# Moving a policy product, four groups of transposes and four stores in a two-layer adaLN/FFN kernel

## The chip, the cores and the metric

The kernel runs on one core of a Trainium2 chip. The metric is the device time of one execution in microseconds (us); less is better. The engines are TensorE (PE; its weight loads are shown as PEld), VectorE (DVE), ScalarE (ACT), GpSimd (POOL) and SyncE (SP). SP, ACT and POOL also issue DMAs from their own queues, each strictly in the order of its program.

## The reference

The input x is 32 sequences of 128 tokens of 512 numbers (4096 tokens), in fp32. Two layers follow each other, `x = x + ffn(cond(x))`, and the part that matters here is the first one and the start of the second:

```
# layer 0, cond: a shared FFN plus the two best of 8 small experts per token
shared = silu(x @ sw1.T) * (x @ sw3.T) @ sw2.T            # 512 -> 1024 -> 512
routed = g0 * expert_a(x) + g1 * expert_b(x)              # gates from a sigmoid router
hid    = (shared + routed) / 3
# layer 0, ffn: one of 8 big experts per sequence, chosen by the last token
logits = gelu(hid[:, -1] @ Wp1 + bp1) @ Wp2 + bp2         # "policy"
sel    = argmax(softmax(logits))
h      = gelu(hid @ W1[sel] + b1[sel]);  out = (h @ W2[sel] + b2[sel]) @ Wo + bo
x1     = x + hid + 0.3 * out
# layer 1, cond: token shift (xk, xr), 16 hashed experts, sigmoid(xr @ w_recept) gate
# layer 1, ffn: a gated recurrence over the 32 sequences' axis, solved step by step
```

## The kernel before

Every fp32 product is made of three products of a split operand: a high part (a cast on ACT) and a low part (a subtraction on DVE). `split` makes the two parts and `mm3` the three products per 128 rows of depth, so PE sees long runs of 12 or 48 products.

The program is traced once, straight on, and a scheduler turns the trace into one fixed order per engine. It takes instructions whose inputs it models as ready, older ones first, so an instruction can move against those that are traced around it. Two means set that order by hand: `tc.issue_after(ins)` puts what is traced within it behind `ins` on the same engine, and a manual dependency of class NoSync does the same for a single pair. Neither adds a wait on the chip.

The tokens come in 32 blocks of 128 (one sequence each), in 8 groups of 4. The stages around the change:

- **Shared FFN, second half** (`shared` over groups 4 to 7, up to 820 us in the trace). For each n = 8 g + c it runs `up(n)`: two runs of 12 products, `p0_n` and `p1_n`, with `mid(n, w)` (here `between`) called after each run; then `down(n - 1)`, then `hook2(g, c)`. `up` sends the sums through ACT and DVE (`sg`, then its split parts `as`), and `down` uses these. `between` and `hook2` place `combine(b)`, which adds a block's shared sum and its two gathered expert rows `o` on DVE (L831, L832), turns the result on PE (four transposes into `pth`), scales it on ACT (L837), stores it (`hid_d` from ACT's queue, `xh_d` from SP's) and keeps the last token's column in `hl`. `get_o` gathers the rows of a later block from POOL's queue, and loads shared sums and x from SP's.
- **Policy, early part.** In `hook2` of the last group's first step (n = 56) `policy(0, 24)` is traced for 24 sequences: product `pol`, Gelu on ACT, a multiplication on DVE (`pr`), a second product `pl` with a matrix of ones that adds over partitions, and then a chain of small DVE operations that sorts the sequences by expert and gives the row indices `idxw` by which POOL gathers the experts' weights (`rawB`). The PSUM pool for `pth`, `pol` and `pl` has one buffer here.
- **End of the shared FFN.** `keep` copies the last group's four sums on ACT (L1053). These four blocks are not combined yet; their sums are stored to `sh_d` (L1056) and read back later.
- **Sequence stage** (820 to 1400 us). Step b runs `up(b+1, "a")` (tiles `pu`), two products `pv` (`send_v`) at every second step, `turn_r(b-1)` (`pr`), `down(b, "a")` (`po`, against W2a), `bend(b+1, "a")` (transposes `pt`, Gelu, split), at the other steps `send_k` (`ptB`), then the same for half b, and every second step `close` (`pb`, the product with Wo, and DVE work). Weights of the next expert are split within a branch that is taken only when a sequence has another expert than the one before. `pt`, `pr`, `ptB`, `pth`, `pol` and `pl` share two PSUM buffers. Three steps apart, `get_o` and then `combine` treat the last four blocks (28 to 31), and three steps later `policy(24, 32)` follows:

```
            late, step = divmod(b - 3, 3)
            if 0 <= late < GB and step == 0:
                with tc.issue_after(last_hid[0]), tc.issue_after(last_w[0]):
                    get_o(NB - GB + late, cb, 1)
...
                with behind(last_split), tc.issue_after(last_turn[0]):
                    if 0 <= late < GB and step == 2:
                        combine(NB - GB + late, ps_t)
                    if late == GB and step == 0:
                        policy(PARTS[0], NB, cb, ps_t)
```

The buffers of `get_o` are single here, so the next block's gathers wait until `combine` has let go of them. `used()` moves the queue of weights on by one: it splits the weights three places ahead and gathers those six places ahead.

The functions that the change touches, with what calls them:

## Time and profile before

| | us |
|---|---|
| median of 3 runs (lowest to highest) | 2436.91 (2435.3 to 2438.0) |
| profiled execution | 2437.49 |
| its span, from the first to the last instruction | 2435.8 |
| busy in the span: PE / PEld / DVE / ACT / POOL | 2399.1 / 2031.1 / 1488.7 / 1079.3 / 413.6 |
| mean granted TensorE clock | 0.997 |
| PE waits in all for: the late `pth` / `pt_0a` / `pl` | 2.5 / 2.2 / 2.1 |

The trace gives, for each engine, the start and length of every instruction in us from the start of the span. In the rows of the timeline, equal neighbours are merged (x12); what stands in brackets is the idle time of that engine just before, and the instruction or DMA that ended it. ACTq and SPq are issues of DMAs from those queues. The granted clock is TensorE's, as a share of full speed.

### The profile page before, as it was taken

The page shows a single profiled execution, that of the slowest core. Times are in us where ns is not written, and L with a number is a line of the kernel's source. Part 1 is how long each engine was busy: PE and PEld are TensorE (multiplying, and loading weights), DVE is VectorE, ACT ScalarE, POOL GpSimd, SP SyncE. Part 2 cuts the span into 40 slices and gives each one's busy share as a digit, 9 for nine tenths or more (in the row PEclk, how much of TensorE's full clock was granted, in tenths as well). Part 3 has the DMA queues.
Part 4 walks back from the last instruction along what each step waited for, and adds up shares of the span by engine and source line. Part 5 has one row for each costly group of instructions (what it writes and reads, how often), then busy time and mean ns, then how long its engine had stood idle before and what let it go on. Part 6 is the DMA issues. An engine that isn't in the chain of part 4 may idle for free.

```text
span 2435.8 us, 36814 instructions
## 1 busy us (share of the span) xinstructions
PE 2399.1 (98%) x12792; PEld 2031.1 (83%) x12792; DVE 1488.7 (61%) x2548; ACT 1079.3 (44%) x1897; POOL 413.6 (17%) x461
## 2 busy tenths in 40 slices
PE   8999999999999999999999999999999999999999
PEld 6788888888888787888888889999988888888887
DVE  8797644456557445446355476767756666666664
ACT  5544633344223545455355466666643233223242
POOL 1000022222233233232222110000010000000012
PEclk9999999999999999999999999999999999999999
DMA  6445555457575234343243287776641111111175
GB/s 214 148 130 171 180 173 165 154 168 256 180 222 185 92 119 138 105 125 115 74 153 131 73 309 230 221 234 225 219 152 61 44 52 50 48 47 48 52 233 182
DMA packets 196382, 357.93 MB, mean 147 GB/s; under 512 B 37664, under 2 KB 70480, under 8 KB 193632
## 3 DMA queue, kind: packets, MB, share of 16 engines
q1 hardware_dynamic: 147648, 257.53, 32.4%
q0 software_dynamic: 36448, 75.95, 10.9%
q10 hardware_dynamic: 12096, 22.03, 2.5%
q8 instruction: 107, 1.75, 0.3%
q14 instruction: 83, 0.68, 0.1%
HBM read 377.08 MB, written 91.80 MB: 192 GB/s over the span
## 4 chain that ended last, share of the span: by engine, by line
PE 51%; DMA 2%; DVE 1%; ACT 1%; issue 0%; POOL 0%; DVEq 0%; ACTq 0%; POOLq 0%
PE phD L82 7%; PE poD L82 7%; PE ps_f L82 7%; PE po L82 4%; PE poF L82 3%; PE ps_c L82 3%; PE pS L82 3%; PE ps_i L82 3%; PE pA L82 2%; PE pb L82 2%; PE pv L82 2%; PE ptD L1431 1%; PE ptC L1599 1%; PE ptF L1574 1%; PE ptB L1256 0%; DMA rawB<-in_W2b_dram,idxw 0%
## 5 line engine op out<-in xcount | busy, mean ns | idle before, releaser
L65 DVE TENSOR_TENSOR wD<-rawD,wD 128x1024 fp32r<-128x1024 f32 x128 | 156.6, 1230 | 82.1 <-ACT wD L64 82.0
L82 PE MATMUL p<-xhl,swu 128*128 128x512 f32 x768 | 190.4, 399 | 5.8 <-ACT xhl L64 5.8
L82 PEld LDWEIGHTS phD<-xe,wD 128*128 128x128 f32 x1536 | 185.1, 189 | 2.2 <-ACT xe L64 1.1
L82 PE MATMUL phD<-xe,wD 128*128 128x256 f32 x1536 | 185.9, 281 | 0.7 <-ACT xe L64 0.7
L82 PE MATMUL p<-xhl,kept_u 128*128 128x512 f32 x768 | 184.3, 394 | 0.7 <-DVE kept_u L65 0.7
L82 PE MATMUL poD<-wD,hD 128*128 128x512 f32 x768 | 181.5, 392 | 0.0
L82 PEld LDWEIGHTS p<-xhl,swu 128*128 128x128 f32 x768 | 145.7, 192 | 36.6 <-ACT xhl L64 5.8
L82 PEld LDWEIGHTS p<-xhl,kept_u 128*128 128x128 f32 x768 | 141.9, 188 | 30.0 <-DVE kept_u L65 1.1
L82 PEld LDWEIGHTS poD<-wD,hD 128*128 128x128 f32 x768 | 141.9, 188 | 28.3
L64 ACT CAST wD<-rawD 128x1024 fp32r<-128x1024 f32 x128 | 133.3, 1046 | 56.4 <-PE poD L82 54.0
L290 POOL DMA_INDIRECT xg<-in_x_rows_dram,blk_t x71 | 67.8, 954 | 446.5 <-PE ptx L300 246.6
L1542 POOL DMA_INDIRECT y<-res_d,gat_i x32 | 35.2, 1100 | 473.4 <-DVE r L1566 389.5
L82 PE MATMUL pur<-r,xb 128*128 x792 | 110.3, 288 | 4.1 <-ACT hbr L64 1.5
L65 DVE TENSOR_TENSOR xb<-ptx,xb 128x512 fp32r<-128x512 f32 x68 | 47.0, 691 | 105.8 <-ACT xb L64 104.1
L82 PE MATMUL por<-r,hbr 128*128 x396 | 108.0, 407 | 1.1 <-ACT hbr L64 1.1
L82 PEld LDWEIGHTS pur<-r,xb 128*128 128x128 f32 x792 | 98.3, 188 | 6.5 <-issue 2.2
L82 PE MATMUL ps_c<-uc_hl,cT 128*128 128x512 f32 x384 | 96.6, 399 | 0.1
L82 PE MATMUL pb<-rT,Wo_hl 128*128 128x256 f32 x768 | 95.2, 281 | 0.3 <-DVE rT L65 0.2
L815 POOL DMA_INDIRECT o<-o_d,s_i x64 | 66.0, 1031 | 170.3 <-PE pth L835 81.2
L82 PE MATMUL acc<-swd,as 128*128 128x512 f32 x384 | 94.2, 391 | 0.2 <-DVE as L65 0.2
L82 PE MATMUL ps_f<-wf_hl,z 128*128 128x512 f32 x384 | 94.4, 394 | 0.0
L82 PE MATMUL pv<-w_recept_hl,xr 128*128 128x512 f32 x384 | 93.1, 391 | 0.0
(1048 smaller groups left out, 5135.3 us busy)
## 6 DMA issues: line engine op xcount, KB each, us to landing
rawD<-in_w_key_dram SPq DMA_DIRECT2D x64, 512.0 KB, 4.1
rawD<-in_w_value_dram SPq DMA_DIRECT2D x64, 512.0 KB, 3.9
swr<-in_sw_dram SPq DMA_DIRECT2D x120, 256.0 KB, 3.5
o_d<-obr SPq DMA_DIRECT2D x66, 256.0 KB, 2.5
rraw<-in_rw_dram SPq DMA_DIRECT2D x32, 256.0 KB, 3.2
xc<-in_x_dram SPq DMA_DIRECT2D x32, 256.0 KB, 3.5
hid_d<-o ACTq DMA_DIRECT2D x32, 256.0 KB, 2.6
xh_d<-xc SPq DMA_DIRECT2D x32, 256.0 KB, 3.1
```

The costliest lines, as they stand in the source:

```text
L64: first = nc.scalar.copy(hi, src).ins
L65: done = nc.vector.tensor_tensor(lo, src, hi.bitcast(F32), ALU.subtract).ins
L82: done = nc.tensor.matmul(ps, lhsT=left(hl, k), rhs=right(hr, k), start=start and k + n == 0, stop=stop and 3 * k + n == last,)
L290: nc.gpsimd.indirect_dma_start(out=xg[i], out_offset=None, in_=a["x_rows"], in_offset=bass.IndirectOffsetOnAxis(ap=blk_t[:, i : i + 1], ax ...
L815: nc.gpsimd.indirect_dma_start(out=o[n], out_offset=None, in_=o_d, in_offset=bass.IndirectOffsetOnAxis(ap=idx[:, b : b + 1], axis=0),)
L1431: nc.tensor.transpose(pt[:, k, :], xe[:, s, bass.ts(k, P)], ident)
L1542: got = nc.gpsimd.indirect_dma_start(out=y, out_offset=None, in_=res_d, in_offset=bass.IndirectOffsetOnAxis(ap=gat_i[:, b : b + 1], axis=0),)
L1574: nc.tensor.transpose(pt[:, k, :], r[:, bass.ts(k, P)], ident)
L1599: nc.tensor.transpose(pt[:, k, :], c[:, bass.ts(k, P)], ident)
```

## The change

Three things are done. The second product of both policies, `pl`, is collected in a list `later`. In the early policy, the list is queued behind the last product of `p1_57`, the second run of the step after policy is traced. In the sequence stage, `hold_back()` follows every `down(b, "a")`, so the late policy's `pl`, and the four transposes of each of the four late `combine` calls (`held=True`), stand on PE behind the product with W2a of the next step. No wait is added on the chip; only PE's order is bound. Third, the four stores of the last group's shared sums are issued from SP's queue instead of ACT's.

The dependency that was written out at the last loop (`last_ob`) becomes a call of the new helper and is the same as before.

```diff
-    last_split = []
+    last_split, last_product, later = [], [], []
+
+    def queue_behind(ins, other):
+
+        tc.add_manual_dep(
+            ins, other.name,
+            mybir.DependencyInfo(mybir.DependencyClass.NoSync, mybir.DependencyReason.DATA),
+            reason="issue_after",
+        )
+
+    def hold_back():
+
+        while later:
+            queue_behind(later.pop(), last_product[0])
...
                     start=start and k + n == 0, stop=stop and 3 * k + n == last,
                 )
+        last_product[:] = [done.ins]
         return done.ins
...
-        def combine(b, ps_t):
+        def combine(b, ps_t, held=False):
...
             for k in range(KD):
-                nc.tensor.transpose(pt[:, k, :], o0[:, bass.ts(k, P)], ident)
+                turned = nc.tensor.transpose(pt[:, k, :], o0[:, bass.ts(k, P)], ident)
+                if held:
+                    later.append(turned.ins)
...
-            mm(pl, ones, pr, True, True)
+            later.append(nc.tensor.matmul(pl, lhsT=ones, rhs=pr, start=True, stop=True).ins)
...
                 if w == 0:
                     sums(*divmod(n - 1, KF))
+                elif n == last * KF + 1:
+                    hold_back()
...
-                        nc.scalar.dma_start(out=sh_d[i * P : (i + 1) * P, :], in_=shs[b])
+                        nc.sync.dma_start(out=sh_d[i * P : (i + 1) * P, :], in_=shs[b])
...
                 down(b, "a")
+                hold_back()
                 used()
...
                     if 0 <= late < GB and step == 2:
-                        combine(NB - GB + late, ps_t)
+                        combine(NB - GB + late, ps_t, True)
```

More of the change, by code (lines that the diff above doesn't have):

```diff
@@ L1703, in tile_kernel @@
         for ob in last_ob:
-            tc.add_manual_dep(
-                ob, last_split[0].name,
-                mybir.DependencyInfo(mybir.DependencyClass.NoSync, mybir.DependencyReason.DATA),
-                reason="issue_after",
-            )
+            queue_behind(ob, last_split[0])
         i0, i1 = (raw_part("wi", h) for h in range(2))
```

## The prediction

> **What bounds the kernel now.** I read the page first, then the waits of PE, then the timeline around each wait that the diff touches, then the windows with the granted clock. The page's first part:

> ```profile
> PE 2399.1 (98%) x12792; PEld 2031.1 (83%) x12792; DVE 1488.7 (61%) x2548; ACT 1079.3 (44%) x1897; POOL 413.6 (17%) x461
> ```

> TensorE is busy for 2399.1 of 2435.8 us, so a change that leaves the products alone can win only idle PE time, 36.7 us in all, and time that PE spends at a lowered clock. The waits of PE (total, times, longest) hold three rows whose instructions the diff moves or relieves:

> ```profile
> PE pth L835 <- DVE o L832: 2.5, 2, 2.3
> PE pt_0a L1151 <- ACT ue_0a L1144: 2.2, 1, 2.2
> PE pl L56 <- DVE pr L865: 2.1, 2, 1.3
> ```

> That is 6.8 us of PE idling. A stop costs a little more than its idle figure, because the last product's tail, which otherwise overlaps the next one, is exposed. So I take each loss from start to start, at the steady price of twelve 512-column products, 2.77 us (0.23 each), and 0.118 for a 256-column one (48 in 5.66), as the chain of waits shows them.

> **The stores of the last shared sums.** The timeline of before, where the shared FFN ends and the sequence stage begins:

> ```profile
> 821.58 3.00 ACTq L1056 DMA_DIRECT2D sh_d<-shc  x2
> ...
> 822.97 1.29 PE L82 MATMUL pu_0b<-wB_W1b,hidhl 128*128 128x512 f32 x5
> ...
> 824.62 1.04 ACT L64 CAST wB_W2b<-rawB 128x1024 fp32r<-128x1024 f32 x1 [2.59 <-DMA hidB<-hid_d]
> ...
> 825.78 0.59 ACT L1144 COPY ue_0a<-pu_0a 128x512 f32<-128x512 f32 x1
> ...
> 826.42 0.66 PE L1151 MATMUL pt_0a<-ident,ue_0a 128*128 128x128 f32 x4 [2.16 <-ACT ue_0a L1144]
> 826.83 3.13 PE L82 MATMUL pu_0b<-wB_W1b,hidhl 128*128 128x512 f32 x7
> ```

> ACT copies the last sum at 822.03. Its fourth store is issued only at 824.26, behind a wait that the landing of a hidB load ends, and in the same queue stand the second half of W2b's cast, then ue_0a, then PE. With the stores on SP, ACT goes on at 822.03: cast to about 823.1, ue_0a to 823.8. PE's five products of pu_0b end at 824.26, so pt_0a finds its input there. PE loses from 822.97 + 5 x 0.23 = 824.12 to 826.42, 2.30 us, and all of it should go.

> A second loss follows it; the windows (PE busy, PEld, DVE, ACT, POOL, granted clock, DMA):

> ```profile
> 824.00:827.00 3.00, 0.84 (x7) 0.58 (x6) 1.23 (x1) 2.24 (x3) 0.00 (x0) 1.00 1.03 371
> 827.00:831.00 4.00, 4.00 (x12) 3.13 (x11) 0.00 (x0) 2.92 (x7) 2.64 (x3) 0.57 0.81 292
> 831.00:835.00 4.00, 4.00 (x21) 3.28 (x20) 1.53 (x3) 2.89 (x8) 1.36 (x2) 1.00 0.23 66
> ```

> The granted clock falls to 0.57 right behind the stop: 4.00 x 0.43 = 1.72 us, and from starts (7 products in 2.93 and 7 in 1.96 instead of 1.61 each) 1.67. I count 1.67 with the stop. Against it: the equal stop at 929 us is followed by a clock of 1.00, so one stop in two has this price, and the term lies between 0 and 1.67; I take the upper end since this execution paid it. [...]

> What SP takes over: four issues of some 0.33 us each, and the wait for a landing. Behind them in SP's queue stand hidB of the third and fourth sequence (issued at 820.43 and 822.11), xB and Wo. The third hidB is cast at 831.01 and used by pu_2a at 842.34; Wo is cast at 850.74. If SP holds until 824.3 instead of 822.1, with 4.5 us to landing, hidB is there at 829. Nothing is lost; if that cover went, each us beyond would cost one.

> **The late sums' transposes.** Four groups lie in the stream of PE, at 929.88, 985.20, 1041.56 and 1096.86. The worst:

> ```profile
> 926.11 1.52 PE L82 MATMUL pv<-w_recept_hl,xr 128*128 128x512 f32 x6
> ...
> 928.99 0.75 DVE L832 SCALAR_TENSOR_TENSOR o<-o,g,o 128x512 f32<-128x512 f32 x1 [0.21 <-DVEq L990]
> ...
> 929.88 0.63 PE L835 MATMUL pth<-ident,o 128*128 128x128 f32 x4 [2.25 <-DVE o L832]
> ...
> 932.10 3.02 PE L82 MATMUL po<-wB_W2a,hb_6a 128*128 128x512 f32 x12
> ```

> From starts: 926.11 + 6 x 0.23 = 927.49 against 929.88, 2.39 lost. At 1041.56 six pv from 1039.78, 0.40; at 985.20 and 1096.86, 36 pb from 980.64 and 1092.30 (4.25 us), 0.31 each. Sum 3.41. The change puts each group behind the next po (W2a): after 935, 993, 1047 and 1105 in the old clock of the trace, where o has been ready for 5 us or more. What comes late with it: ACT's copy, the hid_d and xh_d stores, hl, and the gathers of the next sums, whose single buffers they read. Those gathers land some 40 us before their use at 983, 1039 and 1095, so this is covered; the POOL queue behind them is a rival below. A new price: at the odd steps (985 and 1096) ptB comes straight behind pt in the same two PSUM buffers, and must now wait for ACT's copy of pth: 0.2 us each if ACT (0.60) takes it first, 1.2 if the gelus (1.15) go first. I take 0.4 together, bounds 0 and 2.4.

> **The second products of policy.** Late one:

> ```profile
> 1112.82 3.01 PE L82 MATMUL pu_17a<-wB_W1a,hidhl 128*128 128x512 f32 x12
> ...
> 1117.17 0.43 PE L56 MATMUL pl<-pr,ones 128*128 128x64 f32 x2 [1.35 <-DVE pr L865]
> ...
> 1120.62 3.01 PE L82 MATMUL po<-wB_W2a,hb_16a 128*128 128x512 f32 x12
> ```

> Due at 1112.82 + 2.77 = 1115.59, started at 1117.17: 1.58 lost. It goes behind po_16a, near 1122; its indices then come some 5 us later, and the first weights fetched by them are those of sequence 24, seven steps of about 18 us on. I take the 1.58 whole.

> Early one:

> ```profile
> 760.30 0.59 PE L56 MATMUL pl<-pr,ones 128*128 128x192 f32 x2 [0.76 <-DVE pr L865]
> ```

> 756.57 + 2.77 = 759.34: 0.96 lost. But what follows is DVE's work, and DVE is full:

> ```profile
> 775.00:780.00 5.00, 5.00 (x26) 4.13 (x25) 5.00 (x10) 0.60 (x1) 3.82 (x4) 1.00 0.39 126
> ...
> 781.69 2.12 PEld L82 LDWEIGHTS acc<-kept_d,as 128*128 128x128 f32 x10 [0.24 <-DVE as L65]
> ```

> Policy's chain on DVE starts at 760.93 and ends past 784; the split of as, which acc needs at 781, ends just in time. With pl behind the next p (about 762.3) the chain starts 2 us later, while PE comes 0.96 earlier. So I book 0: the 0.96 is taken at pl and given back at acc. Bounds: +0.96 won if DVE fills the hole with the gating products that wait at 761.98, and 1.5 lost if the chain's whole shift comes through. The first weight gathers (778.30, cast at 792.50) have 10 us to spare less a landing of 4 to 8 us, which covers 2.

> **Sum.** 2.30 + 1.67 + 3.41 + 1.58 + 0 - 0.4 = 8.6 us. The profiled execution took 2437.49 (span 2435.8 and 1.7 around it), 0.6 above the median of the runs. 2437.5 - 8.6 = 2428.9, so 2429.0. What is won stays won as far as the trace shows: from 830 to 1400 PE stands nearly solid, casts wait for PE and not the other way, and the stop at 1421 (rows gathered from what PE produced) moves along.

> **Rivals.** *The clock does not follow the stop.* The half-rate stretch stays, or comes behind another stop: 8.6 - 1.67 = 6.9, 2430.6. For it: the stop of 2.25 us without a drop, and a drop at 103 us with no stop ahead of it; against it, the drop starts within 1 us of the restart. [...]

> *Given back at the next wait.* In the late transposes' places PE meets other late inputs (3.41 gone), and DVE's shift in the early policy costs 1.5: 2.30 + 1.67 + 1.58 - 1.5 = 4.05, 2433.4. For it: DVE at 5.00 of 5.00 there, and a DVE queue that was 2 us behind at 929. Against it: all four groups move to where their input is long ready, and DVE has idle time from 934 on.

> *Slower: weights behind the gathers.* POOL's queue holds the o gathers ahead of rawB gathers (931.93 and 938.09 ahead of 939.35; 986.13 and 989.57 ahead of 991.41). With the transposes up to 8 us later, an o gather at the head of POOL holds the weights 8 us longer. It decides when a rawB gather has less than 8 us between its landing and its cast: then ACT, and with it PE, waits up to 8 us at three places, 24 - 8.6 = 15 us more, 2453. Against it: the casts of new weights in this stretch are only at 911 to 944 and 1076 to 1114, and the o gathers that fall between are far from both.

> **Chances.** Forecast 0.55, clock 0.13, given back 0.22, slower 0.10. A measurement of this kernel tells some 0.2% (4.9 us) from no change. The forecast and the clock case lie below 2432.0: faster 0.68; given back is same, 0.22; slower 0.10. The likeliest case alone runs from 2427 to 2431. Low end: everything won (9.9 us) and the scatter of the runs (about 1.5) gives 2426, taken to 2425.5; high end: the given-back case and its scatter, 2435.0.

> **What would show it.** Right: the three wait rows are gone or under 0.5 us, pt_0a starts within 0.3 of pu_0b's fifth product, the clock is 1.00 from 827 on, pth stands behind po (W2a), acc waits for as by about 0.9 near 780. Wrong: a new PE wait of over 1 us on as, ptB or rawB, or a stop of SP that delays hidhl.

## The result, and the profile after

| | before | after |
|---|---|---|
| median of the runs, us | 2436.92 (7 runs, 2435.3 to 2441.28) | 2430.13 (7 runs, 2427.12 to 2435.3) |
| profiled execution / its span | 2437.49 / 2435.8 | 2429.48 / 2427.8 |

The ratio is 0.9976, with a 95% interval of 0.9965 to 0.9987, so 3.2 to 8.5 us are won; the whole interval lies on the faster side. A repeat beside the last experiments gave 2429.48 against 2436.3, ratio 0.9961 [0.9947, 0.9976]. The forecast was 2429.0.

The engines' row of the page of after:

```profile
PE 2397.2 (99%) x12792; PEld 2030.2 (84%) x12792; DVE 1486.9 (61%) x2548; ACT 1077.9 (44%) x1897; POOL 412.3 (17%) x461
```

PE's busy time fell by 1.9 us for the same 12792 instructions, about the cost of one stretch at half clock (1.7 us behind the stop of before); the rest is idle time. The waits of PE between 740 and 1130 us, the part that the diff touches (total, times, longest):

```profile
PE ptB L1274 <- DVE ps L1200: 1.0, 2, 0.5
PE pt_16a L1169 <- ACT o L853: 0.5, 1, 0.5
PE p L95 <- DVE sg L258: 0.5, 1, 0.5
PE acc L95 <- DVE as L65: 0.2, 1, 0.2
```

The three rows on `pth`, `pt_0a` and `pl` are gone, and the list holds four smaller ones; a `ptB` wait of 0.4 stood in before too. The rows on `sg` and `as` are new and stand in the early policy's stretch. The row `pt_16a` and one of the two `ptB` waits are the price of holding back in the fourth late group.

The stores, in the timeline of after:

```profile
817.93 2.31 SPq L1074 DMA_DIRECT2D sh_d<-shc  x4
...
819.75 1.07 ACT L64 CAST wB_W2b<-rawB 128x1024 fp32r<-128x1024 f32 x1
...
820.50 0.34 SPq L1137 DMA_DIRECT2D hidB<-hid_d  x1
...
821.23 1.07 PE L95 MATMUL pu_0b<-wB_W1b,hidhl 128*128 128x512 f32 x4
821.43 0.59 ACT L1162 COPY ue_0a<-pu_0a 128x512 f32<-128x512 f32 x1 [0.60 <-PE pu_0a L95]
...
822.14 0.60 PE L1169 MATMUL pt_0a<-ident,ue_0a 128*128 128x128 f32 x4
822.50 2.09 PE L95 MATMUL pu_0b<-wB_W1b,hidhl 128*128 128x512 f32 x8
```

SP issues all four stores in 2.31 us, each right behind ACT's copy, without a wait for a landing. ACT is now early: it waits for PE's product (0.60), where before PE waited for ACT. The windows over the same place (PE busy, PEld, DVE, ACT, POOL, granted clock, DMA, GB/s) show the clock at 1.00, where before it was 0.57 behind the stop:

```profile
822.00:825.00 3.00, 3.00 (x17) 2.51 (x16) 0.09 (x1) 2.56 (x7) 2.03 (x3) 1.00 0.83 281
825.00:829.00 4.00, 4.00 (x22) 3.28 (x21) 1.34 (x3) 3.67 (x9) 0.96 (x1) 1.00 0.91 289
```

The first late group in the timeline of after stands behind `po` with no idle time ahead of it:

```profile
923.16 2.88 PE L95 MATMUL po<-wB_W2a,hb_6a 128*128 128x512 f32 x12
925.89 0.60 PE L849 MATMUL pth<-ident,o 128*128 128x128 f32 x4
```

To see where the time came from, I take the distance between the starts of two tiles on PE. The same stretches in every profile but the two with stops made on purpose (us; the starts were read to 0.1, so a difference can be 0.1 off):

| kernel | pol to pu_0a (early `pl`) | pu_0a to pu_2a (stores) | pu_7a to pu_7b (group 1) | pu_13a to pu_13b (group 3) | pu_15b to pu_17a (group 4) | pu_17a to pu_17b (late `pl`) | pol to pu_31b |
|---|---|---|---|---|---|---|---|
| before | 64.4 | 22.1 | 14.7 | 12.8 | 26.4 | 13.7 | 622.6 |
| after | 65.2 | 18.2 | 12.3 | 12.3 | 27.5 | 12.0 | 615.9 |
| after, repeated | 65.0 | 18.1 | 12.3 | 12.3 | 27.5 | 12.0 | 615.6 |
| before + all stores on SP | 67.4 | 18.2 | 16.4 | 12.7 | 26.5 | 13.7 | 623.4 |
| before + early `pl` held | 65.0 | 18.6 | 16.3 | 12.8 | 26.4 | 14.1 | 621.6 |
| before + late groups held | 67.5 | 20.0 | 12.2 | 12.3 | 27.6 | 13.3 | 621.3 |
| before + late `pl` held | 63.8 | 19.9 | 16.3 | 12.8 | 26.4 | 12.0 | 619.6 |
| before + fourth store on SP | 67.2 | 18.3 | 16.3 | 12.8 | 26.5 | 13.7 | 623.2 |
| after + `condS` later | 64.1 | 18.1 | 12.3 | 12.3 | 27.5 | 12.0 | 614.8 |
| after, odd groups not held | 65.0 | 18.2 | 12.2 | 12.3 | 26.4 | 12.1 | 614.7 |
| after, both repairs | 64.0 | 18.2 | 12.2 | 12.3 | 26.5 | 12.0 | 613.7 |

Group 2, from pu_7b to pu_11a, gains 0.1. So the two profiles differ by 0.8 lost at the early `pl`, 3.9 won at the stores, 2.4, 0.1 and 0.5 won in groups 1 to 3, 1.1 lost in group 4 and 1.7 won at the late `pl`: 6.7 won, from `pol` to pu_31b. The profiled executions differ by 8.0, because the execution of after was already 2.6 ahead at `pol`, before any of the change, and lost 1.3 near 2340 us, behind all of it. Those two are no part of the change: a half-clock stretch stands near 103 us in before only, and one near 2340 in after only, and in the other profiles each comes and goes.

### The profile page after: what moved, and what is told of

Same layout as the page of the kernel before. It is cut to its first block, busy times and chain, and to the rows that moved or that the text cites. A ratio compares the mean times of both kernels' runs of the same rounds, so it can differ in the third digit from the quotient of the medians.

```text
span 2427.8 us, 36811 instructions
## 1 busy us (share of the span) xinstructions
PE 2397.2 (99%) x12792; PEld 2030.2 (84%) x12792; DVE 1486.9 (61%) x2548; ACT 1077.9 (44%) x1897; POOL 412.3 (17%) x461
## 4 chain that ended last, share of the span: by engine, by line
PE 76%; DMA 2%; DVE 2%; issue 1%; ACT 1%; ACTq 0%; POOL 0%; DVEq 0%; POOLq 0%
PE phD L95 8%; PE poD L95 7%; PE po L95 7%; PE ps_f L95 7%; PE p L95 6%; PE pb L95 4%; PE poF L95 3%; PE ps_c L95 3%; PE pS L95 3%; PE ps_i L95 3%; PE pv L95 3%; PE acc L95 3%; PE pA L95 2%; PE por L95 2%; PE pur L95 2%
## 5 line engine op out<-in xcount | busy, mean ns | idle before, releaser
L65 DVE TENSOR_TENSOR wD<-rawD,wD 128x1024 fp32r<-128x1024 f32 x128 | 156.5, 1229 | 82.3 <-ACT wD L64 82.3
L64 ACT CAST wD<-rawD 128x1024 fp32r<-128x1024 f32 x128 | 133.5, 1047 | 56.2 <-PE poD L95 54.1
L65 DVE TENSOR_TENSOR xb<-ptx,xb 128x512 fp32r<-128x512 f32 x68 | 46.9, 690 | 106.2 <-ACT xb L64 104.5
L95 PE MATMUL acc<-kept_d,as 128*128 128x512 f32 x384 | 93.4, 391 | 0.9 <-ACT as L64 0.6
```

What stands on the lines that cost most here:

```text
L64: first = nc.scalar.copy(hi, src).ins
L65: done = nc.vector.tensor_tensor(lo, src, hi.bitcast(F32), ALU.subtract).ins
L95: done = nc.tensor.matmul(ps, lhsT=left(hl, k), rhs=right(hr, k), start=start and k + n == 0, stop=stop and 3 * k + n == last,)
```

## Experiments

Each of the first four takes one part of the change alone.

**All four stores on SP, nothing else.**

```diff
-                        nc.scalar.dma_start(out=sh_d[i * P : (i + 1) * P, :], in_=shs[b])
+                        nc.sync.dma_start(out=sh_d[i * P : (i + 1) * P, :], in_=shs[b])
```

> Before, with only the four stores of the last shared sums moved from ACT's queue to SP's. Theory (the stop before pt_0a is ACT held at its fourth store until a hidB load lands): the wait of pt_0a for ue_0a goes from 2.16 us to under 0.3, and from pu_0a to pu_2a PE needs 2.3 us less than the 22.1 us of before, 3.9 less if the half clock behind the stop goes with it. Rival (ACT was late for another reason, the landing of W2b's weights or the copies themselves): the stop stays above 1.5 us. In the total: 2.3 to 3.9 us less, 2433 to 2434.6.

Measured: 2433.4 against 2435.87, ratio 0.9990 [0.9981, 0.9998]. The stretch at the stores took 18.2 instead of 22.1 and the wait of `pt_0a` is gone, as by the theory. The median fell by 2.5, less than 3.9. The profiled execution was the slowest of the twelve (2439.2) and shows what can hide such a gain: the untouched early `pl` and the untouched `pth` both cost more than in the profile of before. PE's waits in this kernel between 740 and 1130 us:

```profile
PE pl L56 <- DVE pr L865: 3.4, 2, 2.1
PE pth L835 <- DVE o L832: 2.5, 2, 2.3
```

`pl` waits 2.1 us at its longest here, against 1.3 before. Each of these stops was followed by a stretch at half clock (764 to 767 and 931 to 934 us).

**The early `pl` alone.** The changed kernel, with the stores back on ACT and the late parts as before:

```diff
-            later.append(nc.tensor.matmul(pl, lhsT=ones, rhs=pr, start=True, stop=True).ins)
+            held = nc.tensor.matmul(pl, lhsT=ones, rhs=pr, start=True, stop=True).ins
+            if b0 == 0:
+                later.append(held)
...
-                        combine(NB - GB + late, ps_t, True)
+                        combine(NB - GB + late, ps_t)
```

> Before, with only the early policy's second product queued behind p1_57. Theory (DVE sets the pace there, and policy's chain on it starts later): the wait at pl (0.76 us) goes, but new waits of PE on DVE near 775 to 790 us take more than it gave; from pol to pu_0a PE needs 0.8 us more than the 64.4 us of before (between 0.5 and 1.5 more). Rival (the 0.8 us that the changed kernel shows there is scatter): 0.96 less than 64.4. The stores are on ACT here, so the stop before pt_0a and perhaps the half clock show again. In the total: 0.8 more, within the scatter.

Measured: 2434.84, ratio 0.9992 [0.9984, 1.0001]. The stretch took 65.0, 0.6 more than in the profile of before. Something not expected: the stop at `pt_0a` shrank from 2.2 to 0.2 although the stores stayed on ACT. In this order ACT's last two stores went out together with no wait, while Wo's loads stood ahead of the second hidB load:

```profile
821.26 0.95 ACTq L1076 DMA_DIRECT2D sh_d<-shc  x2
...
822.12 1.07 SPq L1109 DMA_DIRECT2D raw_Wo<-in_Wo_dram  x2
822.78 1.05 ACT L64 CAST wB_W2b<-rawB 128x1024 fp32r<-128x1024 f32 x1
...
823.83 0.34 SPq L1139 DMA_DIRECT2D hidB<-hid_d  x1
```

In the third and fourth experiments, where the DMAs stand in the order of before, the fourth store was held for 1.7 us and `pt_0a` waited 1.5. So the stop of the kernel before hangs on this order.

**The late groups alone.** The changed kernel with stores on ACT and both `pl` free; `combine(..., True)` stays.

```diff
-            later.append(nc.tensor.matmul(pl, lhsT=ones, rhs=pr, start=True, stop=True).ins)
+            mm(pl, ones, pr, True, True)
```

> Before, with only the four late groups of transposes queued behind the next product with W2a; both second products of policy stay free. Theory (two groups at even steps win their whole stop, two at odd steps meet a shortage of PSUM buffers): 2.4 us less at the first, 0.1 at the second, 0.5 at the third, and at the fourth 0.3 less to 0.8 more, so 2.2 to 3.3 in all from pu_2a to pu_16a's end. Rival (all stops simply go): 3.4 us. Rival (given back at the next wait): under 1 us. Stop and half clock behind the ACT stores as in before.

Measured: 2433.35, ratio 0.9987 [0.9976, 0.9999]. Groups 1 and 3 won 2.5 and 0.5 as in the whole change, group 2 won 0.1 and group 4 lost 1.2. That is 1.9 in all, below the 2.2 to 3.3 expected, because the fourth group lost more than the 0.8 allowed for. The late `pl`, which stays free here, stopped PE for 0.4 less than in before. The free early `pl` met the worst case seen. Its timeline:

```profile
762.14 0.75 DVE L845 SCALAR_TENSOR_TENSOR o<-o,g,shc 128x512 f32<-128x512 f32 x1 [2.77 <-DMA o<-o_d,s_i]
762.81 0.75 DVE L846 SCALAR_TENSOR_TENSOR o<-o,g,o 128x512 f32<-128x512 f32 x1
763.47 0.35 DVE L881 TENSOR_TENSOR pr<-gl,Wp_sb 128x192 f32<-128x192 f32 x1
...
763.88 0.96 PE L56 MATMUL pl<-pr,ones 128*128 128x192 f32 x2 [2.18 <-DVE pr L881]
```

DVE waits 2.77 us for the landing of a row gather, and `pr`, which has nothing to do with that gather, stands behind it in DVE's order and starts only at 763.47. In the profile of before, the same wait was 1.34. How long `pl` stops PE is thus set by a gather's landing, which differs from one profile to the next: the gather is issued 3.4 us ahead of `pol` in each, and its rows were there 2.7 us behind `pol` in before and 4.1 here.

**The late `pl` alone.** As the second experiment, for the other policy.

```diff
+            if b0 > 0:
+                later.append(held)
```

> Before, with only the late policy's second product queued behind the next product with W2a. Theory: the whole 1.58 us between pu_17a and what follows it goes, and nothing new waits: from pu_16b to pu_17b 1.4 to 1.6 us less than the 21.0 of before. Rival (policy's chain, 5 us later, holds up DVE or ACT there, whose loads of activation tables for Exp and Gelu then stand before hf_17a): under 0.7 us. In the total 1.5 us less, within the scatter. Stop and half clock behind the ACT stores as in before.

Measured: 2433.32, ratio 0.9985 [0.9975, 0.9994]. The stretch fell from 13.7 to 12.0 and nothing came back behind it. Here the free early `pl` stopped PE for only 0.4, and `pt_0a` for 1.5 with no fall of the clock.

The four totals together come to 0.46% less, the whole change to 0.24% and, repeated, 0.39%. Each total has an interval of about 0.1% to either side, so the parts are read from the stretches and not from the totals.

**One store.** Is it the fourth store alone that holds ACT?

```diff
-                        nc.scalar.dma_start(out=sh_d[i * P : (i + 1) * P, :], in_=shs[b])
+                        (nc.sync if j == GB - 1 else nc.scalar).dma_start(out=sh_d[i * P : (i + 1) * P, :], in_=shs[b])
```

> Before, with only the fourth of the four stores on SP's queue; the other three stay on ACT's. Theory (one wait, that of the fourth store for an earlier load's landing, holds ACT; the issues themselves, about 0.4 us each, do not): as with all four moved, pt_0a waits under 0.3 us, and PE needs 18.0 to 18.4 us from pu_0a to pu_2a. Rival (ACT is late by its four issues together, some 1.5 us): a stop of 1.0 or more is left and PE needs 19.2 or more.

Measured: 2434.51, ratio 0.9996 [0.9986, 1.0005]; the total can't be told from no change. The stretch can: 18.3, as with all four moved (18.2). Three issues on ACT cost nothing; the wait of the fourth was the whole loss. What exactly ties that issue to the landing of a hidB load was not separated further.

**The early policy's tail, four steps later.** In the changed kernel the last eight DVE operations of the early policy (`condS`, needed only much later) are put off, to see whether DVE is what limits that stretch.

```diff
-            for k in range(KD):
-                by_place(condS[:, k, b0:b1], condT[:, k, b0:b1])
+            def conds():
+                for k in range(KD):
+                    by_place(condS[:, k, b0:b1], condT[:, k, b0:b1])
+
+            return conds
...
+                    if c == 4:
+                        conds[0]()
```

> The changed kernel, with the early policy's last eight DVE operations (the reordered conditions, 6.0 us of DVE) traced three steps later, before the first split of weights, where DVE has idle time. Theory (DVE sets the pace from 762 to 790 us, so the early product's 0.96 us is given back): from pol to pu_0a PE needs 0.5 to 1.8 us less than the 65.2 of the changed kernel, and its waits on sg and as near 775 to 790 us shrink to under 0.5 in all. Rival (PE waits there for something else, ACT's order or PSUM buffers that DVE does not free later): no change, 65.2 within 0.2.

Measured: 2430.44, ratio 0.9976 [0.9966, 0.9986]. The stretch took 64.1 instead of 65.2, and the waits on `sg` and `as` are gone; one of 0.4 on a `pth` of this stretch is new. DVE sets the pace there. The 1.1 us are too few for the totals to show.

**The odd groups free.** In the changed kernel, groups 2 and 4 (steps with a `ptB`) are no longer held.

```diff
-                        combine(NB - GB + late, ps_t, True)
+                        combine(NB - GB + late, ps_t, late % 2 == 0)
```

> The changed kernel, with the second and fourth late groups of transposes (those before odd steps) free as in before, the first and third held as in the change. Theory (held there, pth, pr, pt and ptB share two PSUM buffers at one spot, and pt_16a and ptB wait for ACT and DVE): the waits of pt_10a, pt_16a and ptB (0.4 to 1.0 us at the fourth, none to 0.4 at the second) go, the fourth group's step from pu_15b to pu_17a takes 27.5 less 1.1 = 26.4 us as in before, and the second stays within 0.2. In all 1.0 to 1.3 us less than the changed kernel. Rival (the waits come from DVE's and ACT's weight splits there and stay): under 0.4 us.

Measured: 2430.2, ratio 0.9977 [0.9968, 0.9986]. Group 4 is back at 26.4, the wait of `pt_16a` is gone, and one `ptB` wait of 0.5 stays; group 2 is the same either way. Holding group 4 back costs 1.1 and wins nothing.

**Both repairs, and the change again beside them.**

```diff
+                    if c == 4:
+                        conds[0]()
...
+                        combine(NB - GB + late, ps_t, late % 2 == 0)
```

> The changed kernel with both repairs: the eight VectorE steps on condS of the early policy traced four steps later, and the late combines of odd steps not held. If the two gains found singly are independent, the stretch from pol to pu_0a takes 64.1 us instead of 65.2 and that from pu_15b to pu_17a 26.4 instead of 27.5, so the whole is 2.2 us below the changed kernel, near 2428, a ratio to the kernel before of 0.9967. Rival: VectorE only hands the wait on (pu_0a to pu_2a over 18.2, or the chain past pu_17b longer than 0.3), and the whole stays at the changed kernel's 2430.

> The changed kernel again, beside the repaired one: 2430 us, ratio 0.9976. If the stretches repeat (pol to pu_0a 65.2, pu_0a to pu_2a 18.2, pu_7a to pu_7b 12.3, pu_15b to pu_17a 27.5, each within 0.4), the places of gain and loss are the program's own; if one moves by over 1 us, that place is scatter.

Measured: 2428.76, ratio 0.9962 [0.9947, 0.9976], and 2429.48, ratio 0.9961 [0.9947, 0.9976]. The two gains add up within the stage: from `pol` to pu_31b it took 613.7 against 615.9 and 615.6. The totals don't tell the two kernels apart, so a version that beats the change is shown in its stretches only. The repeat gave every stretch of the change again within 0.2 us. The waits that are left in the repaired kernel between 740 and 1130 us:

```profile
PE ptB L1280 <- DVE ps L1206: 0.5, 1, 0.5
PE pth L849 <- DVE o L846: 0.4, 1, 0.4
```

**Stops of PE by design.** Which stops does half clock follow? In the changed kernel ACT repeats the copy `ue` of seven late steps, which are otherwise free of stops.

```diff
-            nc.scalar.copy(ues[b, half], pu)
+            for _ in range(1 + SLOW.get((b, half), 0)):
+                nc.scalar.copy(ues[b, half], pu)
```

> The changed kernel with stops of seven lengths put into one run: at steps 17, 19, ..., 29 ACT repeats the copy ue (for the first half) 6, 7, 8, 9, 10, 12 and 14 times, and PE's later products are bound behind the transposes pt that need it, so that PE idles by about 1.0, 1.5, 2.1, 2.6, 3.1, 4.2 and 5.3 us. Nothing of the result changes. Theory (seen so far: six of seven stops above 2 us were followed by some 3.5 us at half the granted clock, none of nine up to 1.7): the first two stops are followed by a clock of 1.00, most of those from 2.1 on by about 3.5 us at 0.5. [...]

Measured: 2470.63, with stops of 1.8, 2.5, 3.4, 5.3, 6.5, 5.6 and 6.8 us. The clock stayed at 1.00 behind the first; all six others were followed by half clock. The longest stop in the windows (columns as above):

```profile
1390.00:1392.00 2.00, 0.04 (x1) 0.00 (x0) 0.17 (x1) 1.82 (x4) 0.99 (x1) 1.00 0.07 10
1392.00:1393.00 1.00, 0.00 (x0) 0.00 (x0) 0.00 (x0) 0.97 (x2) 0.00 (x0) 0.79 0.06 1
1393.00:1397.00 4.00, 0.14 (x1) 0.14 (x2) 0.00 (x0) 3.62 (x7) 0.00 (x0) 0.50 0.00 0
1397.00:1401.00 4.00, 4.00 (x14) 3.52 (x15) 0.81 (x2) 2.14 (x6) 0.00 (x0) 0.50 0.12 46
```

PE went idle at 1390.04 and restarted at 1396.86. The clock falls within the stop, at 1392.58, and stays at 0.50 until 1402.81, 6.0 us after the restart.

The second kernel of this kind adds an eighth copy of 16 to 448 columns behind seven full ones, to bring the stops near 2 us.

```diff
+            if (b, half) in SLOW:
+                w = SLOW[b, half]
+                nc.scalar.copy(ues[b, half][:, :w], pu[:, :w])
```

> The changed kernel with seven stops of TensorE made on purpose (ACT repeats the copy ue_a of seven late steps seven times and adds an eighth copy of 16 to 448 columns; no result changes). Six repeats stopped PE 1.8 us without a fall of the clock and seven 2.5 us with one. The new stops should lie between, 2.0 to 2.7 us. [...]

Measured: 2460.29. The two shortest stops in the timeline:

```profile
1138.74 0.66 PE L1173 MATMUL pt_18a<-ident,ue_18a 128*128 128x128 f32 x4 [1.95 <-ACT ue_18a L1166]
...
1177.76 0.66 PE L1173 MATMUL pt_20a<-ident,ue_20a 128*128 128x128 f32 x4 [2.13 <-ACT ue_20a L1166]
```

The stop of 1.95 us left the clock at 1.00. Half clock followed the stop of 2.13 us and the other five (2.2 to 4.4). That looks like an edge at 2.0 us, but length alone doesn't decide it. In the kernel with one store moved, the early `pl` stopped PE for 1.95 us as well, and there the clock fell:

```profile
759.34 0.77 PE L56 MATMUL pl<-pr,ones 128*128 128x192 f32 x2 [1.95 <-DVE pr L865]
```

In these profiles the two differ in where the stop lies. In each profile, every change of the granted clock falls on one grid with steps of 3.413 us. In this run the clock falls at 1178.89, 1219.85, 1260.81, 1301.77, 1346.14 and 1387.10, which are 12, 12, 12, 13 and 12 steps apart, and half clock lasts one, two or three steps (3.41, 6.83 or 10.24 us in the two runs with stops made on purpose). Against the kernel's own events the grid lies differently from profile to profile: the first of 32 small products near 100 us (`ps_z`) starts 0.7 us behind a step of it in before and 2.7 us in after. The windows cut along the grid: four of this run, two of the kernel before at its first late group, and two of the kernel with one store moved:

```profile
1134.52:1137.93 3.41, 2.27 (x10) 1.50 (x8) 2.21 (x5) 3.20 (x7) 2.04 (x2) 1.00 1.00 314
1137.93:1141.34 3.41, 2.60 (x16) 2.29 (x17) 0.00 (x0) 2.63 (x8) 0.99 (x1) 1.00 0.15 46
1175.48:1178.89 3.41, 1.28 (x10) 1.13 (x10) 0.29 (x1) 2.46 (x7) 1.43 (x2) 1.00 0.51 135
1178.89:1182.30 3.41, 3.41 (x9) 2.63 (x8) 1.53 (x4) 1.70 (x5) 0.00 (x0) 0.50 0.21 77
...
926.06:929.47 3.41, 1.57 (x7) 0.95 (x6) 2.03 (x4) 1.88 (x5) 1.26 (x2) 1.00 0.94 308
929.47:932.88 3.41, 3.00 (x17) 2.59 (x18) 1.92 (x6) 1.19 (x2) 2.15 (x3) 1.00 0.69 164
...
756.21:759.62 3.41, 1.46 (x8) 0.92 (x7) 2.02 (x4) 2.95 (x3) 0.00 (x0) 1.00 0.29 87
759.62:763.03 3.41, 3.41 (x10) 2.73 (x10) 1.99 (x5) 0.36 (x1) 0.00 (x0) 0.50 0.00 0
```

PE's idle time in a window is 3.41 less its busy time. The grid cuts the stop of 1.95 us of this run into 1.14 and 0.82, and the clock stays; the first stop of the run with whole copies, 1.8 us, is cut likewise, into 0.97 and 0.80. The stop of 2.13 lies whole in one window, and the next window runs at 0.50. At the first late group of before, the stop of 2.25 us is cut into 1.84 and 0.41, and the clock stays. The stop of 1.95 us at the early `pl` lies whole in one window, and the clock falls. Between 740 and 1400 us in all 13 profiles, the clock fell 20 times, each time at the end of a window in which PE had been idle for 1.95 us or more, and it never fell behind a window with 1.84 or less. So in these profiles the edge lies between 1.84 and 1.95 us of idle time within one window.

## Why the prediction was right, and where its terms were off

**The stores: 2.30 + 1.67 forecast, 3.9 measured.** The mechanism held as put: the fourth issue held ACT, the cast and `ue_0a` stood behind it, and SP took the stores over with no harm (the next hidB load went out at 820.50). That SP might itself be held by the landing did not happen; the bound was not needed. But the term is that of one profile. The other three kernels with all stores on ACT took 18.6, 20.0 and 19.9 for the stretch; the mean of the four, 20.2, is 2.0 above what the change leaves. The 18.6 belongs to another order of the DMAs; without it the mean is 20.7, and 2.5 is won. Beside other executions, then, the part is worth about half to two thirds of what this profile showed.

**The clock behind the stop.** I counted the loss because this execution had paid it, and took "one stop in two" from the two stops I had. The size holds: 3.41 us at half clock cost 1.7. But the two stops were not alike. The one of 2.16 lay whole in one window of the grid (823.66 to 827.07), and the one of 2.25, behind which the clock stayed at 1.00, was cut into 1.84 and 0.41. That the term came in whole rests on where the grid lay in the one profile that I compared with, which is luck. My estimate, with the edge put at 1.9 us between the measured 1.84 and 1.95, is that a stop of 2.2 us has 1.9 in one window for about half of the places at which it can fall, (3.41 + 2.2 - 2 x 1.9) / 3.41 = 0.53; of the nine stops of 1.95 to 2.3 us that no run made on purpose, eight were followed by half clock. The rival, in which the half-rate stretch stays or comes behind another stop, did not come: the clock is 1.00 from 822 to 1414 us in after.

**The late groups: 3.41 - 0.4 = 3.0 forecast, 1.9 measured.** Group 1 won 2.4 (2.39 forecast) and group 3 won 0.5 (0.40). The odd groups were the mis-sized term: each was to win 0.31 and pay 0.2, and group 2 won 0.1 in the net, but group 4 lost 1.1. Its price was 1.4, inside the bound of 2.4 for both and far from the 0.2 I took. The timeline of after shows the two waits:

```profile
1094.85 0.60 PE L849 MATMUL pth<-ident,o 128*128 128x128 f32 x4
...
1096.64 0.66 PE L1169 MATMUL pt_16a<-ident,ue_16a 128*128 128x128 f32 x4 [0.52 <-ACT o L853]
...
1098.01 0.66 PE L1274 MATMUL ptB<-ident,xk 128*128 128x128 f32 x4 [0.47 <-DVE ps L1200]
```

I had looked for one wait, of `ptB` for ACT's copy of `pth`. But `pr` also stands behind `pth` now and takes the second PSUM buffer, so `pt_16a` is the first to need one back, and the copy on ACT that frees the buffer of `pth` stands behind a cast of new W2a weights (1095.05, 1.05 long). `ptB` then waits for the buffer of `pr`, which DVE empties at 1097.27, behind two splits of the same weights (1094.76, 2.59 long). Group 2 falls where no new weights are split, and pays almost nothing. The freed kernel confirms the place: without the hold, the 1.1 is back.

**The late `pl`: 1.58 forecast, 1.7 measured.** Nothing came late with it.

**The early `pl`: 0 forecast, 0.6 to 0.8 lost against the profile of before.** This lies inside the bounds (0.96 won to 1.5 lost), and for the reason given: DVE is full (5.00 of 5.00 us from 775 to 780 in before), and its later start comes through, with 0.5 at `sg` and 0.2 at `as` where I had named about 0.9 at `as`. Putting eight DVE operations off won 1.1, which shows that it is DVE. But the profile of before was a good one for this place. The five profiles with a free early `pl` took 63.8 to 67.5, 66.1 in the mean, and the four with it held and the rest of the early policy unchanged 65.0 to 65.2. So in these profiles the hold wins about 1 us in the mean: it makes the stretch independent of a gather that lands 0 to 2 us late. The mean may lean to the dear side, since the profiled executions of before and of the first five experiments lie 0.6 to 5.8 us above the medians of their kernels. The first weight gathers, to which I gave a landing of 4 to 8 us, took 6.3 to 10.2 between 760 and 800 us in before; the 14.2 us from issue to cast covered that.

**Sum.** 8.6 forecast and 6.7 measured from `pol` to pu_31b. The difference is 0.8 at the early `pl` and 1.1 in the late groups. The forecast, 2429.0, lies 1.1 below the median. It rests on one profile of before, and its odd places came out nearly even, by luck: by the means over the kernels that leave a place as it was, before loses 1.7 more at the early `pl` (66.1 for 64.4) and 1.3 more at `pth` (16.0 for 14.7) than that profile showed, and 2.0 less at `pt_0a`, together 1.0 more. By these few profiles the gain would be about 6.7 + 1.0 = 7.7 us, an estimate within both measured intervals; the medians differ by 6.8.

**The other rivals.** *Given back at the next wait*: part of it came, in group 4 and the early `pl`, 1.9 of the 4.5 it needed. *Weights behind the gathers*: no wait of PE for `rawB` is in the list of after, a cast of new weights holds PE up only by way of the copy of `pth` in group 4, and the stretches between the late groups are those of before.

## What to carry to other kernels

In the profile of before, a stop of TensorE of 2.16 us cost 1.7 us more at half clock, nearly twice its length in all, and one of 2.25 us cost nothing more; the first lay whole in one window of the clock's grid and the second was cut into 1.84 and 0.41. Such a stop is worth removing even where one profile shows it cheap or short. A step that is only ordered later takes its buffer later too (in group 4 the price was 1.4 us): look at which tile takes the next buffer of the pool, and what stands ahead of the copy that frees it, above all where a branch adds work. And compare stretches between two tiles over several profiles before a gain of a microsecond is given to an edit; the total of this kernel varies by more than any single part was worth.
